# Suffix sums from two f16 halves of the values, with the attention stage's emission weights redrawn

## The chip, the cores and the metric

One core of a Trainium2 chip runs the whole kernel in one launch. The metric is the device time of one execution in microseconds (us). The core has five instruction queues, each worked off in its own order: TensorE (PE: matmuls; its weight loads are listed apart as PEld), VectorE (DVE), ScalarE (ACT), GpSimd (POOL) and SyncE (SP, which here only issues DMA transfers).

## What is computed

One decoder layer on 4 x 1024 tokens of width 512 (16 heads of 32): gated causal self-attention, a retention block on a second input, and a feed-forward block with simulated int8 quantisation, each followed by a residual sum and a layernorm. The change lies in the self-attention:

```python
scores = jnp.einsum('bhqd,bhkd->bhqk', Q, K) / scale
scores = jnp.where(causal[None, None], jnp.asarray(-1000000000.0, x.dtype), scores)
...                                        # head_gates: two small softmaxes of the mean of x
scores = scores * head_gates[:, :, None, None]
attn = jax.nn.softmax(scores, axis=-1)
out = jnp.einsum('bhqk,bhkd->bhqd', attn, V)
```

A masked score is -1e9 times a gate, not minus infinity. When a gate is tiny, the masked (future) keys keep a weight that is the same for all of them, so the kernel needs, beside the ordinary attention, the sum of V over all future keys of each query: the suffix sum of the values.

## The kernel before, in words

The kernel has three stages. In the trace, attention runs to about 1035 us, the retention block follows, and the feed-forward block closes. Only attention is edited.

Attention works in 16 units: 4 batches x 4 groups of 128 channels (4 heads). For each unit:

- **Projection** (`proj_qk` and `proj_v`, from line 554): K, Q and V as three f16 matmuls each (high x high, high x low, low x high; the helper `mm3g`, lines 193 to 199). V is kept in f32, in eight tiles of 128 tokens x 128 channels (line 602). High and low f16 halves of Q and K go to DRAM and come back stacked for the score matmuls (`kst`, `qst`, lines 583 and 591, by SP).
- **Coarse sweep** (`coarse`, lines 620 to 648): scores with f16 halves (`pco`), their maxima by DVE (line 637); one small matmul (`pnm`, line 643) turns the maxima round, and a DMA puts them into `qst` as an extra row, so that the main sweep subtracts them.
- **Suffix sums** (`suffix`, lines 604 to 618): for each pair of token tiles, one f32 matmul per tile with the V tile as weights against `tri_f`, a 128 x 129 triangle of ones with a column of ones at its end (line 611). ACT then adds the running total of the later tiles, tile by tile (line 616), so that each tile waits for the one behind it.
- **Main sweep** (`main`, from line 658), in two halves of 512 queries (g = 0, 1): scores (`pst`, line 703), exponentials on ACT (line 707), product with V (`av`, line 688), and a running sum of the exponentials, mostly on POOL and in some key tiles on DVE (line 693). `corr` (lines 675 to 683) weighs the suffix sums with E, the weight of a masked key; POOL does the product at line 683. The epilogue `ep1` (from line 726) turns the running sum into denominators (`pd`, line 730).

The stage's PSUM tiles take eight banks: three double-bank tiles `st`, shared by `pco`, `pnm`, `pst` and the `pe` of `corr`; one bank `av`; and one bank `mm`, shared by the projections (`pqk`, `pv`), the suffix sums (`psuf`), the output projection (`po`) and the denominators (`pd`).

The order of the work is set in two steps. The Python code runs five generators side by side (`merge`, line 934): `mains`, `coarses` (coarse sweep, then suffix, one unit ahead of `mains`), `all_oprojs`, `others` (sums of x, weights, gates) and `projs`. A generator yields a cost after each piece; the merge always advances the one with the least cost so far divided by its weight (`W_MAIN`, `W_CO`, `W_OP`, `W_X`, `W_PR`). Some yields are only delays (`D_C0` before the first coarse sweep, `D_CO` before each later one, `D_NM` before `pnm`), `C0F` speeds up the first sweep, and `EP1` is how many empty turns stand ahead of an epilogue (line 748). The framework then lays out each engine's queue from that emission order, by its own estimate of when an instruction is ready (`schedule_with_timeline_sim=True`). Engines meet only through semaphores.

The start (`first`, line 774) projects units 0 and 1 and ends with the suffix sums of unit 0.

Of the kernel before, what the change touches and what calls it, by code (L numbers as in the profile page):

```python
# [8 lines left out]
F32 = mybir.dt.float32  # L9
F16 = mybir.dt.float16  # L10
# [3 lines left out]
ALU = mybir.AluOpType  # L14
# [4 lines left out]
P = 128  # L19
B, L, D, H, HD = 4, 1024, 512, 16, 32  # L20
KC = D // P
NT = L // P
# [25 lines left out]
HB = 1  # L48
LOP = "kq"
XLP = 0  # L50
EP1 = 2
D0 = (2,3)
DS = ((), ())
DD = (3,)
# [9 lines left out]
W_OP = 13360.0  # L64
W_OPL = 7700.0
W_CO = 10400.0
D_CO = 1377.0
MTQ = 0
X1Q = 0
ATLP = 0  # L70
NRB = 4
X_S = 215.2
OT = 1
D_C0 = 3876.0
C0F = 4.309
WBY = 250
X_P = 151.7
D_NM = 163.1
W_PR = 20760.0
W_G = 8800.0  # L80
W_X = 10160.0
W_S = 10250.0
W_BE = 11480.0
W_F = 2293.0
W_S1 = 33600.0
# [24 lines left out]
def scaled(gen, f):  # L110
    for cost in gen:
        yield cost / f
# [25 lines left out]
def decoder_kernel(ctx: ExitStack, tc: tile.TileContext, a, c, out):  # L138
    nc = tc.nc
# [95 lines left out]
    xp = ab.enter_context(tc.tile_pool(name="a_x", bufs=1))  # L235
# [113 lines left out]
    with ExitStack() as es:  # L349
        cp = es.enter_context(tc.tile_pool(name="a_c", bufs=1))  # L350
        wk_ = es.enter_context(tc.tile_pool(name="a_w", bufs=2))
        ps = es.enter_context(tc.tile_pool(name="a_ps", bufs=2, space=PSUM))
        st = {}

        def prep(b):
# [3 lines left out]
            for j in range(2):  # L359
                for k in range(KC):  # L360
# [4 lines left out]
                    (nc.gpsimd if XLP else nc.vector).tensor_tensor(out=s["xl"][:, k, tk], in0=xf, in1=s["xh"][:, k, tk], op=ALU.subtract)  # L365
                    yield X_P

# [40 lines left out]
        bo = cp.tile([P, D], F32, name="bo")  # L408
        cnt = cp.tile([P, 2, 16], F32, name="cnt")
        hsel = cp.tile([P, KC, H], F32, name="hsel")  # L410
        tri_f = cp.tile([P, P + 1], F32, name="tri_f")
        future = cp.tile([P, P], BF16, name="future")
        ident_m = cp.tile([P, P], F32, name="ident_m")
        nc.vector.tensor_scalar_mul(ident_m, ident, -1.0 / MS)
# [12 lines left out]

        def consts():
            trib = xp.tile([P, P], F32, tag="xf", name="trib", bufs=2)
            for t, src in (  # L430
                (bsel, c["bsel"]),
                (hsel, c["hsel"]),
                (bq, a["bq"].rearrange("(o p) -> p o", p=P)),
                (tri_f, c["tri"]),
                (trib, c["trib"]),
                (cnt, c["cnt"]),
                (bv, a["bv"].rearrange("(o p) -> p o", p=P)),
                (bo, a["bo"].rearrange("(o n) -> o n", o=1).to_broadcast([P, D])),
            ):
                nc.sync.dma_start(out=t, in_=src)  # L440
            nc.vector.tensor_scalar_mul(future, trib, -1e30)

        g_qs, g_qb, g_gc = (cp.tile([P, B, KC], F32, name=f"g_q{i}") for i in range(3))
        g_gn = cp.tile([P, B, H], F32, name="g_gn")
# [9 lines left out]
        def xsums(b):  # L454
            xs = xp.tile([P, KC, 2], F32, tag="xs2", name="xs2", bufs=2)
            for k in range(KC):
                for j in range(2):
                    xf = xp.tile([P, 512], F32, tag="xf", name="xf", bufs=2)
                    nc.sync.dma_start(out=xf, in_=a["xT"][k * P:(k + 1) * P, b * L + j * 512:b * L + (j + 1) * 512])
                    nc.scalar.activation(xf, xf, AF.Copy, accum_out=xs[:, k, j:j + 1])  # L460
                    yield X_S
            nc.vector.tensor_tensor(out=xsum[:, :, b], in0=xs[:, :, 0], in1=xs[:, :, 1], op=ALU.add)
# [122 lines left out]
        def stack_q(n, g):  # L585
            if len(qst_) < min(n + 1, 2):
                qst_.append(xp.tile([97, 2, 4, 512], F16, tag=f"qst{n}", name=f"qst{n}"))
            b, ot = divmod(n, KC)
            qst = st[b]["qst", ot] = qst_[n % 2]
            for j, w in enumerate((0, 1, 0)):  # L590
                nc.sync.dma_start(out=qst[32 * j:32 * j + 32, g], in_=split_rows("q", n)[w, :, :, g * 512:(g + 1) * 512])

        def proj_v(b, ot):
# [3 lines left out]
            for g in range(2):  # L597
# [3 lines left out]
                    yield from mm3g(p[:, t, :], [lambda k, x_=x_: x_[:, k, tk] for x_ in (s["xh"], s["xl"])], [lambda k, w_=w_: w_[:, k, cs] for w_ in wv], KC, 56)  # L601
                nc.scalar.activation(v[:, 4 * g:4 * g + 4, :], p, AF.Copy, scale=1.0 / WS)

        def suffix(b, ot):
            s = st[b]
            v = s["v", ot]
            suf = s["suf", ot] = xp.tile([P, NT, P + 1], F32, tag="suf", name="suf", bufs=2)
            for t0 in range(NT - 2, -1, -2):
                p = ps.tile([P, 2, P + 1], F32, tag=SUF, name="psuf", bufs=BANKS[SUF])
                for t in range(2):  # L610
                    nc.tensor.matmul(p[:, t, :], lhsT=v[:, t0 + t, :], rhs=tri_f, start=True, stop=True)
                for t in (1, 0):
                    if t0 + t == NT - 1:
                        nc.scalar.copy(suf[:, t0 + t, :], p[:, t, :])
                    else:
                        nc.scalar.activation(suf[:, t0 + t, :], p[:, t, :], AF.Identity, bias=suf[:, t0 + t + 1, P:])
                yield 220
            ready.add((b, ot))

        def coarse(b, ot):  # L620
            s = st[b]
            qst, ks = s["qst", ot], s["kst", ot]
            for half in range(2):
                m = wk_.tile([P, 4, 4, 3], F32, tag="m", name="m", bufs=2)
                nc.scalar.copy(m[:, :, :, 2], gt[b]["gn"][:, 4 * ot:4 * ot + 4].unsqueeze(2).to_broadcast([P, 4, 4]))
                for i in range(4):
                    qt = 4 * half + i
                    for h in range(0, 4, 2):
                        for part in range(1 + half):
                            n = min(512, P * (qt + 1) - 512 * part)  # L630
                            p = ps.tile([P, 2, 512], F32, tag="st", name="pco", bufs=NST)
                            for j in range(2):
                                nc.tensor.matmul(p[:, j, :n], lhsT=qst[0:96, half, h + j, i * P:(i + 1) * P], rhs=ks[0:96, h + j, 512 * part:512 * part + n], start=True, stop=part < half)  # L633
                            if part == half:
                                for j in range(2):
                                    nc.tensor.matmul(p[:, j, n - P:n], lhsT=ident_b, rhs=future, start=False, stop=True)  # L636
                            nc.vector.tensor_reduce(out=m[:, h:h + 2, i, 1 - half + part], in_=p[:, :, :n], axis=AX.X, op=ALU.max)  # L637
                            yield 2 * n * 0.42
                m16 = wk_.tile([P, 4, 4], F32, tag="nm", name="m16", bufs=2)
                nc.vector.tensor_reduce(out=m16, in_=m[:, :, :, 1 - half:], axis=AX.X, op=ALU.max)  # L640
                yield D_NM
                pt = ps.tile([16, P], F32, tag="st", name="pnm", bufs=NST)
                nc.tensor.matmul(pt, lhsT=m16.rearrange("p h t -> p (h t)"), rhs=ident_m, start=True, stop=True)
                mt = wk_.tile([16, P], F16, tag="mt", name="mt", bufs=2)
                nc.scalar.copy(mt, pt)
                (nc.scalar if MTQ else nc.sync).dma_start(out=qst[96:97, half].rearrange("o h (t n) -> o (h t) n", n=P), in_=mt)
                yield 60
                ready.add((b, ot, half))
# [9 lines left out]
        def main(b, ot):  # L658
# [4 lines left out]
            for g in range(2):  # L663
# [83 lines left out]

                pend.extend([lambda: 0] * EP1 + [ep1])
                need[ep1] = (b - 1, 4 * g + 4) if ot == 0 and b else None
# [15 lines left out]
        def unit(n):  # L765
            return divmod(n, KC)
# [7 lines left out]
        def first():  # L774
            yield from proj_qk(0, 0, "k")
            stack_k(0)
            g = hidden0()
            next(g)
            yield from proj_qk(0, 1, "k")
            stack_k(1)  # L780
            for k in range(KC):
                split(wv[0][:, k], wv[1][:, k], wvst[:, k], WS)
            next(g)
            wqst = stage("acc", 2, "wqst")
            nc.sync.dma_start(out=wqst, in_=a["wqT"].rearrange("(k p) n -> p k n", p=P))
            consts()
            yield from proj_v(0, 0)
            for _ in g:
                pass
            split(wq[0], wq[1], wqst, WS)  # L790
            yield from proj_v(0, 1)
            yield from proj_qk(0, 0, "q")
            stack_q(0, 0)
            stack_q(0, 1)
            yield from proj_qk(0, 1, "q")
            stack_q(1, 0)
            stack_q(1, 1)
            yield from suffix(0, 0)

        def second():  # L800
# [5 lines left out]
        def weights_o():  # L806
            for k in range(KC):
                wst = xp.tile([P, 512], F32, tag="xf", name="wst_o", bufs=2)
                nc.sync.dma_start(out=wst, in_=a["woT"][k * P:(k + 1) * P])
                split(wo[0][:, k], wo[1][:, k], wst, WS)  # L810
                yield X_S
            clips()
# [74 lines left out]
        def coarses():  # L887
            yield D_C0
            yield from scaled(coarse(0, 0), C0F)
            for n in range(1, NA):  # L890
                yield from until("main", n - 1)
                yield from until("proj", n + 1)
                if n > 1:
                    stack_k(n)
                    if n == 2:
                        stack_q(n, 0)
                    stack_q(n, 1)
                yield D_CO
                yield from coarse(*unit(n))
                yield from suffix(*unit(n))  # L900

# [50 lines left out]
    with ExitStack() as es:  # L952
        pool = lambda nm: es.enter_context(tc.tile_pool(name=nm, reuse_waits="tile", bufs=2))
        wk_, hp, cp = pool("b_w"), pool("b_h"), pool("b_c")
# [232 lines left out]
    with ExitStack() as es:  # L1187
        cp = es.enter_context(tc.tile_pool(name="c_c", reuse_waits="tile", bufs=1))
        wk_ = es.enter_context(tc.tile_pool(name="c_w", reuse_waits="tile", bufs=2))
# [239 lines left out]
```

## Time and profile before

| what | value |
|---|---|
| time before, median of 3 runs | 1973.27 us (1962.6 to 1976.05) |
| profiled execution, its own time | 1978.85 us |
| its span in the trace | 1977.1 us (1.75 us lie around it) |
| mean granted TensorE clock | 0.979 |
| PE busy | 1832.6 us, 93% of the span, 13456 matmul records |
| DVE / ACT / POOL busy | 1455.4 / 918.2 / 1015.4 us (74 / 46 / 51%) |
| suffix matmuls | 128 instructions, 256 records (f32 leaves two records each) |

PE's records overlap: a `pv` matmul is listed with 0.22 us, and the next one starts 0.06 us after it. So the cost of a matmul on PE is read from the start of one record to the start of the next, not from its duration.

### The profile page before, as it was taken

The page shows a single profiled execution, that of the slowest core. Times are in us where ns is not written, and L with a number is a line of the kernel's source. Part 1 is how long each engine was busy: PE and PEld are TensorE (multiplying, and loading weights), DVE is VectorE, ACT ScalarE, POOL GpSimd, SP SyncE. Part 2 cuts the span into 40 slices and gives each one's busy share as a digit, 9 for nine tenths or more (in the row PEclk, how much of TensorE's full clock was granted, in tenths as well). Part 3 has the DMA queues.
Part 4 walks back from the last instruction along what each step waited for, and adds up shares of the span by engine and source line. Part 5 has one row for each costly group of instructions (what it writes and reads, how often), then busy time and mean ns, then how long its engine had stood idle before and what let it go on. Part 6 is the DMA issues. An engine that isn't in the chain of part 4 may idle for free. (4 is left out here: it accounts for less than half of the span.)

```text
span 1977.1 us, 34827 instructions
## 1 busy us (share of the span) xinstructions
PE 1832.6 (93%) x13456; PEld 968.2 (49%) x13456; DVE 1455.4 (74%) x2455; ACT 918.2 (46%) x1496; POOL 1015.4 (51%) x962
## 2 busy tenths in 40 slices
PE   7689899999999999998889999999999999799996
PEld 4444445444445444554434555555555555344432
DVE  4567766677766777678886777787777767798888
ACT  5655555555555555555553323333223322454375
POOL 1075566756667656766553455445554545200066
PEclk9899999999999999999999999999999999899999
DMA  9612222212123112223137454454545444561076
GB/s 272 192 45 67 82 73 68 84 60 81 54 68 97 62 55 65 73 81 129 44 95 223 136 149 139 147 158 134 153 143 150 120 120 144 176 231 34 0 240 229
DMA packets 149720, 231.00 MB, mean 117 GB/s; under 512 B 34479, under 2 KB 58674, under 8 KB 148914
## 3 DMA queue, kind: packets, MB, share of 16 engines
q1 hardware_dynamic: 148978, 227.72, 38.0%
q8 instruction: 106, 1.74, 0.4%
q10 hardware_dynamic: 576, 1.05, 0.1%
q14 instruction: 60, 0.49, 0.1%
HBM read 156.89 MB, written 71.70 MB: 116 GB/s over the span
## 5 line engine op out<-in xcount | busy, mean ns | idle before, releaser
L693 POOL TENSOR_TENSOR acc<-acc,pt 128x384 f32<-128x384 f32 (+3 forms) x436 | 441.0, 1042 | 244.5 <-ACT pt L707 146.2
L637 DVE TENSOR_REDUCE m<-pco 128x2 f32<-128x1024 f32 (+3 forms) x384 | 356.9, 950 | 128.5 <-PE pco L636 71.3
L707 ACT ACTIVATE pt<-pst 128x1024 f32<-128x1024 f32 (+3 forms) x320 | 240.6, 766 | 179.5 <-PE pst L706 102.4
L633 PE MATMUL pco<-kst,qst 96*128 96x512 f16 (+3 forms) x768 | 186.0, 332 | 28.6 <-DMA qst<-qhl_d 15.7
L703 PE MATMUL pst<-qst,kst 97*128 97x512 f16 (+3 forms) x768 | 187.6, 331 | 9.1 <-DVE m L637 4.9
L1324 POOL TENSOR_TENSOR r<-r,xt 128x512 f32<-128x512 f32 x28 | 38.4, 1383 | 196.2 <-DVE r L1321 186.6
L688 PE MATMUL av<-pt,v 128*32 128x512 f32 (+3 forms) x1280 | 131.0, 482 | 8.7 <-ACT pt L707 7.9
L633 PEld LDWEIGHTS <-qst 96*128 96x128 f16 x768 | 63.7, 99 | 120.2 <-issue 83.7
L1059 POOL TENSOR_TENSOR rs<-var,neghalf 128x16 f32<-128x16 f32 x32 | 93.6, 2925 | 46.9 <-DVE var L1057 26.4
L703 PEld LDWEIGHTS <-kst 97*128 97x128 f16 x768 | 59.4, 98 | 104.0 <-issue 83.2
L1253 PEld LDWEIGHTS <-slab_c 128*128 128x128 bf16 x704 | 68.3, 98 | 78.4 <-issue 1.4
L196 PE MATMUL pqk<-xh,slab_a 128*128 128x512 f16 x256 | 97.1, 384 | 8.7 <-ACT xh L399 5.9
L693 DVE TENSOR_TENSOR acc<-acc,pt 128x512 f32<-128x512 f32 (+3 forms) x102 | 96.5, 963 | 8.7 <-POOL acc L693 4.7
L197 PE MATMUL pqk<-xl,slab_a 128*128 128x512 f16 x256 | 98.0, 383 | 0.0
L198 PE MATMUL pqk<-xh,slab_a 128*128 128x512 f16 x256 | 97.8, 382 | 0.0
L196 PE MATMUL pkv<-slab_b,ch 128*128 128x512 f16 x256 | 97.0, 379 | 0.4 <-DVE dn L732 0.4
L197 PE MATMUL pkv<-slab_b,ch 128*128 128x512 f16 x256 | 97.0, 379 | 0.0
L198 PE MATMUL pkv<-slab_b,cl 128*128 128x512 f16 x256 | 97.0, 379 | 0.0
L1256 ACT ACTIVATE sl<-pw_gate,sgx 128x512 f32<-128x512 f32 x88 | 60.1, 684 | 76.3 <-PE pw_gate L1253 74.7
L196 PE MATMUL pv<-slab_a,xh 128*128 128x128 f16 x512 | 92.0, 221 | 3.4 <-ACT slab_a L170 2.4
L197 PE MATMUL pv<-slab_a,xh 128*128 128x128 f16 x512 | 92.0, 221 | 1.2 <-DVE slab_a L171 1.2
L1020 DVE TENSOR_TENSOR sm<-pst,cmask 128x512 f32<-128x512 f32 x128 | 85.3, 679 | 10.5 <-PE pst L1018 9.2
(299 smaller groups left out, 4595.7 us busy)
## 6 DMA issues: line engine op xcount, KB each, us to landing
xt<-x_d SPq DMA_DIRECT2D x63, 256.0 KB, 3.1
xf<-in_xT_dram SPq DMA_DIRECT2D x48, 256.0 KB, 2.8
kst<-khl_d SPq DMA_DIRECT2D x48, 256.0 KB, 4.0
qst<-qhl_d SPq DMA_DIRECT2D x96, 128.0 KB, 3.8
sk<-qhl_d SPq DMA_DIRECT2D x48, 256.0 KB, 3.8
sk<-khl_d SPq DMA_DIRECT2D x48, 256.0 KB, 4.0
khl_d<-khl SPq DMA_DIRECT2D x16, 512.0 KB, 2.8
xr<-in_x_dram SPq DMA_DIRECT2D x32, 256.0 KB, 2.7
```

Of the source, the lines that this page charges most:

```text
L196: nc.tensor.matmul(ps, lhsT=lh(k), rhs=rh(k), start=k == 0, stop=False)
L197: nc.tensor.matmul(ps, lhsT=lh(k), rhs=rl(k), start=False, stop=False)
L198: nc.tensor.matmul(ps, lhsT=ll(k), rhs=rh(k), start=False, stop=k == n - 1)
L633: nc.tensor.matmul(p[:, j, :n], lhsT=qst[0:96, half, h + j, i * P:(i + 1) * P], rhs=ks[0:96, h + j, 512 * part:512 * part + n], start=True ...
L637: nc.vector.tensor_reduce(out=m[:, h:h + 2, i, 1 - half + part], in_=p[:, :, :n], axis=AX.X, op=ALU.max)
L688: together(nc.tensor.matmul(av[32 * h:32 * h + 32, lo:], lhsT=v[:, kt, 32 * h:32 * h + 32], rhs=pt[:, h, lo:], start=kt == 0, stop=kt == n ...
L693: last["acc"] = eng.tensor_tensor(out=acc[:, h:h + hb, lo:], in0=acc[:, h:h + hb, lo:], in1=pt[:, h:h + hb, lo:], op=ALU.add)
L703: nc.tensor.matmul(p[:, j, lo:], lhsT=ks[:, h + j, kt * P:(kt + 1) * P], rhs=qst[:, g, h + j, lo:], start=True, stop=kt < 4 * g)
L707: last[kt] = nc.scalar.activation(pt[:, h:h + 2, lo:], p[:, :, lo:], AF.Exp)
L1020: nc.vector.tensor_tensor(out=sm, in0=pst, in1=cmask[:, None, :].to_broadcast([P, 4, P]), op=ALU.mult)
L1059: nc.gpsimd.tensor_tensor(out=rs, in0=var, in1=neghalf, op=ALU.pow)
L1253: nc.tensor.matmul(p, lhsT=wT[nm][:, k, i * P:(i + 1) * P], rhs=xqT[g][:, k, :], start=k == 0, stop=k == KC - 1)
```

## The change

The values are split once per unit into a high f16 half (ACT copy) and the remainder in f16 (POOL subtraction), and the suffix matmuls run twice in f16, accumulating in the same bank, against an f16 triangle. `halves` is emitted ahead of the coarse sweep of its unit, and in the start just ahead of the suffix sums of unit 0. The triangle is loaded in f32 into the two-buffer ring `xf`, which the sums of x use too, and copied to f16 by DVE. `vs` has one buffer. Beside it, the merge's costs, delays and weights are redrawn, and one empty turn ahead of each epilogue goes. Nothing uses `W_S`; the other constants are used in the attention stage alone.

```diff
-EP1 = 2
+EP1 = 1
...
-D_CO = 1377.0
+D_VS = 41.83
+D_CO = 1322.0
...
-X_S = 215.2
+X_S = 245.7
...
-D_C0 = 3876.0
-C0F = 4.309
+D_C0 = 6395.0
+C0F = 6.75
...
-X_P = 151.7
-D_NM = 163.1
-W_PR = 20760.0
+X_P = 120.4
+D_NM = 147.5
+W_PR = 19130.0
...
-W_X = 10160.0
-W_S = 10250.0
+W_X = 16350.0
+W_S = 1801.0
...
-        tri_f = cp.tile([P, P + 1], F32, name="tri_f")
+        tri_h = cp.tile([P, P + 1], F16, name="tri_h")
...
             trib = xp.tile([P, P], F32, tag="xf", name="trib", bufs=2)
+            tri = xp.tile([P, P + 1], F32, tag="xf", name="tri", bufs=2)
...
-                (tri_f, c["tri"]),
+                (tri, c["tri"]),
...
+            nc.vector.tensor_copy(tri_h, tri)
...
+        def halves(b, ot):
+            s = st[b]
+            v = s["v", ot]
+            vs = s["vs", ot] = wk_.tile([P, 2, NT, P], F16, tag="vs", name="vs", bufs=1)
+            for g in range(2):
+                tg = slice(4 * g, 4 * g + 4)
+                nc.scalar.copy(vs[:, 0, tg], v[:, tg])
+                nc.gpsimd.tensor_tensor(out=vs[:, 1, tg], in0=v[:, tg], in1=vs[:, 0, tg], op=ALU.subtract)
+                yield D_VS
+
         def suffix(b, ot):
...
-                    nc.tensor.matmul(p[:, t, :], lhsT=v[:, t0 + t, :], rhs=tri_f, start=True, stop=True)
+                    for i in range(2):
+                        nc.tensor.matmul(p[:, t, :], lhsT=vs[:, i, t0 + t, :], rhs=tri_h, start=i == 0, stop=i == 1)
...
             stack_q(1, 1)
+            yield from halves(0, 0)
             yield from suffix(0, 0)
...
                 yield D_CO
+                yield from halves(*unit(n))
                 yield from coarse(*unit(n))
                 yield from suffix(*unit(n))
```

More of the change, by code (lines that the diff above doesn't have):

```diff
@@ L602, in proj_v @@
                 nc.scalar.activation(v[:, 4 * g:4 * g + 4, :], p, AF.Copy, scale=1.0 / WS)
+        def halves(b, ot):
[7 more added lines that the diff above has]
+                yield D_VS
         def suffix(b, ot):
             s = st[b]
-            v = s["v", ot]
+            vs = s["vs", ot]
             suf = s["suf", ot] = xp.tile([P, NT, P + 1], F32, tag="suf", name="suf", bufs=2)
```

## The prediction

> **What bounds the kernel now.** I read the busy times by stage first, to see which engine fills the attention stage (the only one edited); then PE's own waits in it; then the order of time around suffix matmuls, for their price; and last the rows that price the new work on ACT and POOL. The busy times by stage, cut at the start of the first coarse sweep and at the end of attention (columns: stretch, length, PE, PEld, DVE, ACT, POOL busy, granted clock, DMA share, GB/s):
>
> ```profile
> 48.00:61.00 13.00, 1.03 (x11) 0.87 (x10) 2.39 (x5) 7.58 (x17) 0.00 (x0) 0.68 0.89 229
> 61.00:75.00 14.00, 13.62 (x70) 7.84 (x68) 10.68 (x15) 6.64 (x18) 0.00 (x0) 0.81 0.61 197
> 75.00:1035.00 960.00, 898.34 (x7246) 453.57 (x7245) 691.18 (x998) 526.67 (x878) 610.42 (x615) 0.99 0.25 75
> ```
>
> From 75 to 1035 us PE is busy 94% of the time, DVE 72%, POOL 64%, ACT 55%. PE's waits in that stretch are short (who waited for whom: total, times, longest), and all 28 rows together make 58.6 us:
>
> ```profile
> PE pnm L643 <- DVE m L640: 10.3, 8, 3.6
> PE av L688 <- ACT pt L707: 7.9, 18, 1.5
> ...
> PE pco L633 <- DMA kst<-khl_d: 5.3, 6, 1.4
> ...
> PE pco L633 <- DMA qst<-qhl_d: 3.7, 2, 2.0
> ...
> PE pd L730 <- DVE acc L693: 2.4, 3, 1.1
> ...
> PE psuf L611 <- ACT suf L616: 2.3, 3, 1.8
> ...
> PE pd L730 <- POOL acc L693: 0.8, 1, 0.8
> ```
>
> So attention is a queue of matmuls with few holes: a microsecond taken out of PE's queue comes off the end, unless it turns into a new hole. The price of a suffix pair (two tiles, four records) and of a small f16 matmul, from PE's order of time (start, us, group):
>
> ```profile
> 440.35 0.66 PE L611 MATMUL psuf<-tri_f,v 128*128 128x129 f32 x4
> 440.84 0.60 PE L633 MATMUL pco<-kst,qst 96*128 96x512 f16 x2
> ...
> 541.23 0.22 PE L196 MATMUL pv<-slab_a,xh 128*128 128x128 f16 x1
> 541.29 0.22 PE L197 MATMUL pv<-slab_a,xh 128*128 128x128 f16 x1
> 541.34 0.22 PE L198 MATMUL pv<-slab_a,xl 128*128 128x128 f16 x1
> 541.40 0.22 PE L196 MATMUL pv<-slab_a,xh 128*128 128x128 f16 x1
> ```
>
> From start to start the f32 pair takes 440.84 - 440.35 = 0.49 us; one f16 matmul of 128 columns with weights of its own takes (541.40 - 541.23)/3 = 0.056 us. The start-up (same columns):
>
> ```profile
> 47.65 0.61 PE L611 MATMUL psuf<-tri_f,v 128*128 128x129 f32 x4
> 60.23 0.37 PE L633 MATMUL pco<-kst,qst 96*128 96x128 f16 x2 [11.97 <-DMA qst<-qhl_d]
> ```
>
> Here one pair of unit 0 lies in front of a wait of 11.97 us for a transfer, and costs nothing.
>
> **The suffix matmuls, units 1 to 15.** 15 units x 4 pairs = 60 pairs. Each goes from 0.49 us to four f16 matmuls, 4 x 0.056 = 0.22 (129 columns as against 128 adds nothing I can read). 60 x 0.27 = 16.2 us off PE's queue. Lower bound: the start-to-start of a record inside the group, (440.84 - 440.35)/4 = 0.12 us, may hold some 0.01 us of switching to the next group; with 0.45 per pair the gain is 13.8. Upper: 0.50 per pair (a second pair stands from 564.56 to 565.06) gives 16.8.
>
> The Trainium skill speaks against this price: "TensorE: Matmul & The Clock Gate", section "Back-to-back issue gap", gives about 81 ns per matmul as the sustained spacing at 128 columns once each has its weight load, and 56 ns only for the isolated gap. By 81 ns the pair would cost 0.32 and the gain would be 60 x 0.17 = 10 us. The row of this trace has weights of its own for each `pv` matmul and still shows 0.056, so the row stands.
>
> **Unit 0.** Pairs 2 and 3 run at the low clock of the second row above (0.81), 0.96 us each (61.68 to 62.64 and 64.14 to 65.10 in the same order of time), pair 4 takes 0.50: 2.4 us outside the wait. In the built queue of the changed kernel two pairs stand ahead of the first coarse matmul, not one; the other two cost 2 x 0.22 to 2 x 0.45. Gain 1.7 us (0 if the wait shrinks with it).
>
> **ACT.** 32 copies of 128x512 from f32 to f16. The row of the same shape is 0.61 us:
>
> ```profile
> L567 ACT CAST khl<-qk 128x512 f16<-128x512 f32 x27 | 16.5, 612 | 0.2
> L568 POOL TENSOR_TENSOR khl<-qk,khl 128x512 f16<-128x512 f32 x26 | 32.1, 1233 | 38.5 <-ACT khl L567 38.5
> ```
>
> 32 x 0.61 = 19.5 us on an engine that is 55% busy. But place matters. `vs` has one buffer, so the copies of unit n+1 need the last suffix matmul of unit n, and in the built ACT queue both copies stand as a pair just before the last additions of unit n's totals, with exponentials next behind. The single `mm` bank comes free, and the exponentials run, up to 1.22 us later. Behind the suffix pair, PE has score or value matmuls that do not need that bank. Bounds: 0 (all hidden) to 19.5 us (each copy in full). I take 5, nearer to 0, because PE waited for the suffix additions 3 times in 60 (2.3 us) and for exponentials 7.9 us in all.
>
> **POOL.** 32 subtractions x 1.23 us = 39 us on an engine 64% busy. In the built queue the two of a unit stand together, 24 or more coarse tiles ahead of the first suffix matmul that reads them, so PE does not wait for them. Who stands behind them: the weighting of the previous unit's suffix sums (line 683), Q and K remainders and the running sums. Exponentials of 1024 wait for PE (lines 703 and 706), and in this stretch for POOL only once, 1.4 us, so the pool of `pt` buffers has slack. I take 0; if that cover went, each pair would hold `pt` or a denominator back by up to 2.5 us. As a bound I add 3 us (the 3.2 us that PE waits for the running sum at `pd`, once more).
>
> **Triangle.** The load has the same 128x129 f32; DVE gets one copy of it, less than the 0.69 us of its 128x512 f16 rows, once, beside PE. The transfer now goes through the `xf` ring, and in the built SP queue the first load of x for the sums stands behind both triangles and two weight loads, the next ones behind more stack loads. ACT takes these sums in turn with Q's halves, whose store and load end the 11.97 us wait. A load of x lands 3.0 us after its issue: the wait can end 3 us earlier or later. I take 0.
>
> **The redrawn weights.** All units are emitted in another order; no row prices that directly. From the built PE queues I counted matmuls (without suffix) between two events, which needs no time. From the last value product of a half to its denominators: more in 18 of 32 cases, fewer in 10; places with under 10 in between go from 9 to 5 of the 32, and the least from 2 to 4, although the empty turn is gone (`EP1`). From the last coarse tile to `pnm`: two places with 0 become 4; longer in three more units (up to 60). From the last score matmul of unit n-2 to the coarse sweep that needs its buffers: 24 to 39 before, 24 to 79 after. On the other side the suffix ends later against the next coarse sweep (some of its tiles stand ahead of the last pair in 10 units, 7 before), so `corr` gets its totals later. `D_CO` plus two `D_VS` is 1405.7 against 1377: nothing. Bounds: all waits for `pnm`, `pd` and the stack loads gone, 10.3 + 3.2 + 5.3 + 3.7 = 22.5 us off, or as much again on. I take 4 off: the 3.2 at `pd` and some of `pnm`.
>
> **The sum.** -16.2 - 1.7 + 5 + 0 + 0 - 4 = -16.9, say -17. The profiled execution took 1978.85 us, so 1962 there; it lies 5.6 above the median of 1973.27, and against the median the forecast is 1956.3 us. The retention and feed-forward stages are not edited; only their queues shift by readiness.
>
> **The rivals.**
> A, the forecast: PE's saving arrives, the rest nearly cancels. Own range 1948 to 1966 (ACT 0 to 10, redraw -8 to 0).
> B, the redraw also closes holes: three quarters of the 22.5 us go. -17.9 - 16.9 + 5 = -30: 1943.5. For it: the counts above. Against: half of the holes come from DVE and DMA, which lose no work.
> C, the saving is given back on ACT: every copy delays the exponentials in full. -17.9 - 4 + 19.5 = -2.4: 1971. For it: the place of the pair in the queue. Against: ACT is idle 45% of the stage, mostly waiting for PE.
> D, slower: the same pair of copies holds the only `mm` bank and one exponential behind it, and PE's next matmul on that bank stands at the head of its queue. Price per unit 1.22 + 1.02 (an exponential of 1024) = 2.24 us, x 15 = 33.6; -17.9 - 4 + 33.6 = +11.7: 1985. It decides from (17.9 + 4)/15 = 1.5 us per unit on. Against: PE has other matmuls to run between.
>
> **How the numbers follow.** A 0.50, B 0.22, C 0.19, D 0.09. A measurement of this kernel tells about 1% (19.7 us) from no change: under 1953.5 is faster, above 1993 slower. Faster: nearly all of B (0.20) and the lower part of A (0.16), 0.36. Slower: the part of D whose price passes 2.8 us per unit, and a start-up or redraw at its upper bound, 0.06. Within: 0.58. The range 1938 to 1980 holds A, most of B and C, and leaves out D above 1980 and the redraw at its full lower bound with the copies hidden (-17.9 - 22.5 = 1933).
>
> **What would show it.** Right: suffix records start 0.056 us apart and their PE busy time shrinks; attention ends about 17 us earlier; PE's waits stay near 59 us; the subtractions are never what `psuf` waits for. Wrong: `psuf` 0.08 us or more apart; new waits of PE for `suf` or `pt` near the copies, of 1 us per unit (C) or over 1.5 (D); a wait before the first `pco` that is 3 us longer or shorter; or retention and feed-forward differing by more than 3 us.

## The result, and the profile after

The changed kernel takes **1987.52 us** (median of 5 runs, 1984.42 to 1992.52). Against runs of before on the same chip the ratio is 1.0087 (95% interval 1.0066 to 1.0107): 0.9% slower, some 17 us (the two medians, 1973.27 and 1987.52, lie 14 us apart). The forecast was 1956.3 us, and the range ended at 1980. The profiled execution of after took 1984.42 us; that of before, 1978.85, lies 8 us above the medians of before beside the experiments (1969.3 to 1971.5 us), so two single traces are compared with care below.

The busy line of the page of after:

```profile
PE 1822.1 (92%) x13432; PEld 950.2 (48%) x13456; DVE 1472.6 (74%) x2456; ACT 931.6 (47%) x1528; POOL 1048.5 (53%) x994
```

PE lost 10.5 us of busy time; some of it is not saved but missing, since 24 matmul records fewer are listed, and the last stage, where nothing was edited, lacks about as many. ACT and POOL, which got the copies and the subtractions, gained 13.4 and 33.1 us. The line to notice is DVE: 17.2 us more (1455.4 before), with one instruction more. Something made DVE's old instructions last longer.

Busy times by stage, after (same columns as before, attention now ends at 1047):

```profile
48.00:61.00 13.00, 0.69 (x6) 0.32 (x3) 2.85 (x5) 7.95 (x20) 0.00 (x0) 0.62 0.70 207
61.00:75.00 14.00, 10.89 (x65) 6.33 (x66) 11.02 (x14) 6.34 (x15) 3.24 (x2) 0.86 0.64 206
75.00:1047.00 972.00, 893.42 (x7256) 438.53 (x7254) 707.13 (x1001) 539.29 (x907) 638.45 (x644) 0.98 0.24 74
```

In attention PE is busy 5 us less than before and the stretch is 12 us longer. PE's waits in it, over all rows, are some 77 us, where they were 58.6. Summed by the engine that ended them, those for DVE grew most, from 25.9 to 39.0 us; those for ACT went from 22.4 to 29.1. The largest:

```profile
PE pnm L657 <- DVE m L654: 11.7, 9, 2.3
PE av L702 <- ACT pt L721: 11.4, 19, 2.8
PE pst L717 <- DVE m L651: 7.3, 15, 1.1
PE pco L647 <- DVE m L651: 5.7, 16, 1.0
```

No row stands out as a new wait: matmuls of the main and coarse sweeps wait a little more often for exponentials and for DVE's maxima. The suffix matmuls cost what was forecast, 65.45 - 65.23 = 0.22 us per pair (order of time on PE):

```profile
65.23 0.39 PE L625 MATMUL psuf<-tri_h,vs 128*128 128x129 f16 x4
65.45 0.38 PE L647 MATMUL pco<-kst,qst 96*128 96x512 f16 x1
```

Behind attention, where nothing was edited, this trace of after is 6.5 us shorter than that of before (935.6 against 942.1 us). The prediction had named a difference of more than 3 us there as a sign of being wrong. Two traces can differ by that without a cause in the change: with the same queues, the stretch of 475 us behind attention took 472.1 us in e14 below and 480.6 in e15.

### The profile page after: what moved, and what is told of

Its sections match the earlier page's. It is cut to its first block, busy times and chain, and to the rows that moved or that the text cites. A ratio compares the mean times of both kernels' runs of the same rounds, so it can differ in the third digit from the quotient of the medians.

```text
span 1982.6 us, 34876 instructions
## 1 busy us (share of the span) xinstructions
PE 1822.1 (92%) x13432; PEld 950.2 (48%) x13456; DVE 1472.6 (74%) x2456; ACT 931.6 (47%) x1528; POOL 1048.5 (53%) x994
## 3 DMA queue, kind: packets, MB, share of 16 engines
q10 hardware_dynamic: 576, 1.05, 0.1%
## 5 line engine op out<-in xcount | busy, mean ns | idle before, releaser
L707 POOL TENSOR_TENSOR acc<-acc,pt 128x384 f32<-128x384 f32 (+3 forms) x436 | 433.5, 1024 | 186.9 <-ACT pt L721 172.6
L707 DVE TENSOR_TENSOR acc<-acc,pt 128x1024 f32<-128x1024 f32 (+3 forms) x102 | 105.2, 1044 | 10.2 <-POOL acc L707 7.0
L1036 DVE TENSOR_TENSOR sm<-pst,cmask 128x512 f32<-128x512 f32 x128 | 85.2, 681 | 10.5 <-PE pst L1034 10.2
```

Source lines behind the costliest of these rows:

```text
L707: last["acc"] = eng.tensor_tensor(out=acc[:, h:h + hb, lo:], in0=acc[:, h:h + hb, lo:], in1=pt[:, h:h + hb, lo:], op=ALU.add)
L1036: nc.vector.tensor_tensor(out=sm, in0=pst, in1=cmask[:, None, :].to_broadcast([P, 4, P]), op=ALU.mult)
```

## The experiments

First came the parts of the change and prices of single operations, each with the queues that the framework lays out for it. They contradicted each other, and the layout itself turned out to move the time (e11 and e15); the last six therefore hold before's queues. In the cuts from the code, the bookkeeping around a call is left out. Ratios are to before on the same chip.

### Which part costs: halves or weights

```diff
 # e1: the halves, and all old constants
-D_CO = 1322.0
+D_CO = 1377.0 - 2 * D_VS
 # e2: f32 suffix sums as before, and all new constants
-D_CO = 1377.0
+D_CO = 1322.0 + 2 * 41.83
 # e3: the changed kernel with two empty turns
-EP1 = 1
+EP1 = 2
 # e4: the changed kernel with the old D_C0, C0F, W_X and X_S
```

> The f16 halves and the f16 suffix matmuls with every emission constant of the kernel before (the delay ahead of a coarse sweep is 1377 less the two costs that the halves yield, so the merge places the same pieces as before). Theory R (the redrawn order is what cost time): the suffix saving of 14 to 16 us arrives here, 1955 to 1962 us against 1973. Theory H (the halves' work on ACT and POOL is what cost time, the order is neutral): about as slow as the changed kernel, 1983 to 1990 us.

> The f32 suffix matmuls of the kernel before with every emission constant of the changed kernel (the delay is 1322 plus the two costs that the halves yield). Theory R: the order alone costs 25 to 30 us, so 1998 to 2003 us. Theory H: near the kernel before, 1968 to 1978 us.

> The changed kernel with two empty turns ahead of an epilogue again, all else as changed. Theory R with the denominators at fault: most of the loss comes back, 1965 to 1975 us. Theory R with another constant at fault, or theory H: within 4 us of the changed kernel, 1983 to 1991 us.

> The changed kernel with the four constants of the start and of the sums of x as before (first delay, speed of the first coarse sweep, weight of the other work, cost of a sum of x). Theory R with the start at fault: the 10 us by which the first masked-key weights came later go away, 1975 to 1979 us. Otherwise within 4 us of the changed kernel.

| run | median us | ratio (95%) |
|---|---|---|
| e1: halves, old constants | 1984.95 | 1.0072 (1.0056 to 1.0087) |
| e2: f32, new constants | 1970.38 | 1.0001 (0.9989 to 1.0013) |
| e3: changed kernel, two turns | 1979.53 | 1.0046 (1.0032 to 1.0061) |
| e4: changed kernel, old start | 1991.72 | 1.0103 (1.0086 to 1.0119) |

The redrawn weights alone change nothing that can be measured. The halves are slower in all four orders of emission (e1, the change itself, e3, e4), by 9 to 20 us.

### What in the halves costs

```diff
 # e5: old constants; halves made once, all units read unit 0's
-            vs = s["vs", ot]
+            vs = st[0]["vs", 0]
 # e6: old constants; halves made and not read
-                    for i in range(2):
-                        nc.tensor.matmul(p[:, t, :], lhsT=vs[:, i, t0 + t, :], rhs=tri_h, start=i == 0, stop=i == 1)
+                    nc.tensor.matmul(p[:, t, :], lhsT=s["v", ot][:, t0 + t, :], rhs=tri_f, start=True, stop=True)
 # e7: e1 without the subtraction, one f16 matmul per tile
 # e8: e1 with the subtraction on DVE
-                nc.gpsimd.tensor_tensor(out=vs[:, 1, tg], in0=v[:, tg], in1=vs[:, 0, tg], op=ALU.subtract)
+                nc.vector.tensor_tensor(out=vs[:, 1, tg], in0=v[:, tg], in1=vs[:, 0, tg], op=ALU.subtract)
 # e9: e1 with the copies on POOL
-                nc.scalar.copy(vs[:, 0, tg], v[:, tg])
+                nc.gpsimd.tensor_copy(vs[:, 0, tg], v[:, tg])
```

> Old emission constants, f16 suffix matmuls, but the halves are made once, for unit 0, and all 16 units multiply unit 0's halves (their suffix sums are those of unit 0; the rest is computed in full). So PE has the f16 price and ACT and POOL have 30 copies and 30 subtractions less. Theory P (PE bounds attention, the work on ACT and POOL is what cost time): the saving of 14 to 16 us arrives, 1955 to 1958 us against 1971. Theory F (the shorter suffix is worth nothing or less, since PE's queue only gets more holes or a lower clock): 1969 to 1985 us.

> Old emission constants, the f32 suffix matmuls of the kernel before, and the 32 copies and 32 subtractions as work whose output nobody reads. Theory P: PE does all it did, and the copies and subtractions cost their full 28 to 30 us, 1998 to 2002 us. Theory F: the same work costs little, 1971 to 1978 us. In between, both have a part.

> Old emission constants, f16 suffix from the high half alone: 32 copies on ACT, no subtraction, one f16 matmul per tile (the remainder of the values is left out of the suffix sums). Theory POOL (the subtractions are what cost time): 1948 to 1958 us. Theory ACT (the copies are): within 8 us of the f16 halves at old constants, 1976 to 1985 us.

> Old emission constants, f16 halves, the subtraction on DVE (0.69 us a piece by its rows) in place of POOL (1.16 us). Theory POOL: most of the loss goes, 1958 to 1972 us. Theory ACT: 1980 to 1990 us, since the copies stay and DVE, at 72% of the stage, gets 22 us more.

> Old emission constants, f16 halves, both the copies and the subtractions on POOL, none on ACT. Theory A (the 19.5 us of copies on ACT are what cost time, and PE's saving is worth nothing): 1970 to 1976 us against 1971. Theory W (any new link between V and the suffix costs it, on whatever engine): 1980 to 1986 us.

| run | median us | ratio (95%) |
|---|---|---|
| e5: halves once | 1973.92 | 1.0009 (0.9988 to 1.0029) |
| e6: halves unread | 1981.22 | 1.0065 (1.0041 to 1.0089) |
| e7: high half only | 1983.81 | 1.0082 (1.0054 to 1.0110) |
| e8: subtraction on DVE | 1978.90 | 1.0058 (1.0035 to 1.0080) |
| e9: copies on POOL too | 2000.97 | 1.0161 (1.0140 to 1.0183) |

e5 is the first surprise: the saving on PE, taken nearly alone, is worth nothing. e9 suggests that work is dearest on POOL: in its trace the stack loads of K came late, and PE's largest wait is

```profile
PE pco L647 <- DMA kst<-khl_d: 21.4, 10, 2.7
```

But e7 adds no work to POOL at all and is as slow as e1, which speaks for ACT's copies.

### Is PE, or ACT, the bound

```diff
 # e10: before, each f32 suffix matmul twice
-                    nc.tensor.matmul(p[:, t, :], lhsT=v[:, t0 + t, :], rhs=tri_f, start=True, stop=True)
+                    for i in range(2):
+                        nc.tensor.matmul(p[:, t, :], lhsT=v[:, t0 + t, :], rhs=tri_f, start=i == 0, stop=i == 1)
 # e11: before, one ACT copy per pair in place of the two chained additions
+                nc.scalar.copy(suf[:, t0:t0 + 2, :], p)
 # e12: e2 with EP1 = 2
```

> The kernel before with every f32 suffix matmul run twice into the same bank (the suffix sums come out doubled): 128 more f32 matmuls, 29 to 31 us of PE time, nothing else. If attention were bound by PE's queue: 1996 to 2002 us. If PE has room at these places, as the halves made once suggest: 1971 to 1980 us. In between, PE binds in one direction: added time counts, time taken away doesn't.

> The kernel before with one ACT copy per suffix pair in place of two chained additions (the running totals over token tiles are left out): 64 instructions in place of 128, some 18 to 22 us less on ACT, PE as before. Theory A in its strong form (ACT binds attention both ways): 1956 to 1962 us. If ACT's additions were covered and only the place of the copies costs: 1967 to 1972 us.

> The f32 suffix with the redrawn constants, but two empty turns ahead of an epilogue. The return of the second turn was worth 8 us to the changed kernel. If that gain belongs to the order alone: 1962 to 1966 us, faster than both kernels. If it belongs to the halves (their pair on ACT near the denominators): 1968 to 1973 us.

| run | median us | ratio (95%) |
|---|---|---|
| e10: suffix twice | 2006.74 | 1.0180 (1.0163 to 1.0197) |
| e11: one copy per pair | 1988.38 | 1.0084 (1.0060 to 1.0108) |
| e12: f32, new constants, two turns | 1968.53 | 0.9985 (0.9972 to 0.9998) |

Time added on PE arrived (some 30 us of matmuls, 36 us of end); time taken off it did not (e5). And e11, which takes work off ACT and adds none anywhere, costs 17 us. No theory of a busy engine explains that. What e11 shares with e1 and e7 is that the framework laid out its queues anew. So up to here each run had two causes in it, its work and its layout; that goes for e10's 36 us too.

### The same queues

For these six, every instruction that before also has keeps before's place on each of the five queues. An edge that orders two instructions of one engine, without a wait, ties each to its predecessor in before's queue:

```diff
+    for e, steps in order.items():          # before's queue of engine e
...
+            tc.add_manual_dep(k, before.name, mybir.DependencyInfo(mybir.DependencyClass.NoSync, mybir.DependencyReason.DATA), reason="the same queues")
+            before = k
```

Only added instructions stand between them: the second f16 matmul behind the first, the copies and the subtractions, in e13's places (e16 has its own). The f32 triangle keeps a tile of its own beside the f16 one.

> The halves of the change with all old constants, as in the first experiment, but with every instruction that before also has held in before's order on each of the five queues; only the added copies, subtractions and second matmuls stand between them (the f32 triangle keeps a tile of its own). Against 1971 us of before. Theory L (the loss comes from the queues being laid out anew, not from the work): the saving on PE arrives less the small delays of ACT, 1956 to 1966 us. Theory W (the halves' own work costs it, whatever the order): 1982 to 1988 us, as in the first experiment.

> As in the experiment with the halves made once (only unit 0's halves are made, and all units use them, so the suffix sums of the other units are wrong), but with before's order held on each queue. This is the saving on PE alone. Theory L: 13 us less than before, 1955 to 1961 us, since nothing but the suffix matmuls changes. Theory W': PE's time at the suffix matmuls is not what sets the end, so 1970 to 1974 us again.

> As in the experiment with one ACT copy per suffix pair (the running totals are left out), but with before's order held on each queue. It takes about 20 us of ACT work away and a chain of waits. Theory L: 1966 to 1972 us, no slower than before. Theory W'': the timing of ACT alone throws the engines against each other, and it stays at 1985 us or more.

> Before's f32 suffix sums, and the halves made but read by nothing, with before's order held on each queue: the price of the added work of ACT and POOL alone. Theory L: 1971 to 1976 us (the 5 us that the prediction gave ACT, or less). Theory W: 1980 to 1984 us, as without held queues.

Two further runs split e13, in its places:

```diff
 # e17: copies for all units, subtractions for unit 0 alone
+                if (b, ot) == (0, 0):
+                    nc.gpsimd.tensor_tensor(out=once[:, tg], in0=v[:, tg], in1=vs[:, tg], op=ALU.subtract)
 # e18: subtractions for all units, copies for unit 0 alone
+                if (b, ot) == (0, 0):
+                    nc.scalar.copy(once[:, tg], v[:, tg])
+                nc.gpsimd.tensor_tensor(out=vs[:, tg], in0=v[:, tg], in1=once[:, tg], op=ALU.subtract)
```

> The halves with before's order held on each queue, and with ACT's copies in the same places as there, but POOL's subtractions made for unit 0 alone: the other units read unit 0's low half, so their suffix sums are wrong. Beside the run with halves made once (1969.6 us, no copies and no subtractions) and the one with all halves (1987.7 us, both) this is the corner with copies alone. Theory S (a copy pair delays PE by about 0.6 us at its place, and POOL's subtractions make DVE's small addition to the denominators last up to 4 us in three places): 15 x 0.6 = 9 us over the corner without either, 1976 to 1981 us, and no such addition over 1.5 us. Theory C (the copies are all of it): 1985 us or more. Theory N (neither alone): 1970.

> The other corner: POOL's subtractions for every unit in the same places, ACT's copies for unit 0 alone, whose high half the other units read and subtract (their suffix sums are wrong). Theory S: the three long additions of DVE stay (3.7 to 4.0 us where they last 0.2 to 0.7 without the subtractions), each with the wait of PE behind it, 3 x 3 = 9 us and what half clock adds: 1978 to 1983 us. Theory C: 1970 to 1972 us, subtractions hidden.

| run, before's queues | ACT copies | POOL subtractions | suffix | median us | ratio (95%) |
|---|---|---|---|---|---|
| e14: halves once | unit 0 | unit 0 | f16 | 1969.63 | 1.0004 (0.9987 to 1.0021) |
| e17: copies only | all | unit 0 | f16 | 1972.97 | 1.0018 (1.0003 to 1.0033) |
| e18: subtractions only | unit 0 | all | f16 | 1984.29 | 1.0087 (1.0064 to 1.0111) |
| e13: halves | all | all | f16 | 1987.66 | 1.0093 (1.0069 to 1.0117) |
| e16: halves unread | all | all | f32 | 1977.39 | 1.0037 (1.0020 to 1.0055) |
| e15: one copy per pair | none | none | f32 | 1970.03 | 0.9999 (0.9982 to 1.0016) |

Three things are settled by this table.

**The layout alone moves the time by as much as the change.** e15 issues the same instructions as e11 and takes 17 to 18 us less. So e7, and every comparison of two layouts, can't be read as a price.

**POOL's subtractions are most of the loss.** They cost 14.7 us without the copies (1984.29 - 1969.63) and 14.7 us with them (1987.66 - 1972.97). These pairs of runs stand on different chips (e13, e14 and e17, e18); by the ratios to before on each chip it is 16 and 15 us, with some 6 us of uncertainty. The copies cost 3.3 us by the medians and 1 to 3 by the ratios, which is not clear of the noise. Theory S named the right part: e18 came out 1.3 us above its range, and e17 3 us below, since it put the copies too high (9 us).

**The saving on PE is worth nothing even when nothing else changes** (e14). For Theory L this was the miss: it had 1955 to 1961.

How a subtraction on POOL reaches the end, in the traces. DVE's small addition that completes the denominators (a tile's row: count, then least, median and longest duration in ns), in before, e14, e18 and the changed kernel:

```profile
L733 DVE TENSOR_TENSOR dn<-dn,ec x32: 150/176/1036, 112.5 to 1036.4; 128x16 f32<-128x16 f32 x32
```

```profile
L748 DVE TENSOR_TENSOR dn<-dn,ec x32: 150/176/886, 110.7 to 1032.2; 128x16 f32<-128x16 f32 x32
```

```profile
L751 DVE TENSOR_TENSOR dn<-dn,ec x31: 151/176/3968, 111.6 to 1010.7; 128x16 f32<-128x16 f32 x31
```

```profile
L747 DVE TENSOR_TENSOR dn<-dn,ec x31: 147/175/2392, 116.8 to 1015.9; 128x16 f32<-128x16 f32 x31
```

The same 128x16 instruction lasts 0.18 us or 3.97 us. One of the long ones in e18, in DVE's order of time and, below it, POOL's:

```profile
511.94 3.97 DVE L751 TENSOR_TENSOR dn<-dn,ec 128x16 f32<-128x16 f32 x1
515.84 0.70 DVE L699 TRANSPOSE_TENSOR_REDUCE ec<-E 128x16 f32<-128x512 f32 x1
516.46 0.20 DVE L752 RECIPROCAL dn<-dn 128x16 f32<-128x16 f32 x1
516.60 0.62 DVE L655 TENSOR_REDUCE m<-pco 128x2 f32<-128x512 f32 x1
```

```profile
505.20 2.27 POOL L617 TENSOR_TENSOR vs<-v,once 128x512 f16<-128x512 f32 x2
507.43 2.38 POOL L711 TENSOR_TENSOR acc<-acc,pt 128x256 f32<-128x256 f32 x5
509.76 1.17 POOL L571 TENSOR_TENSOR khl<-qk,khl 128x512 f16<-128x512 f32 x1
510.88 3.87 POOL L711 TENSOR_TENSOR acc<-acc,pt 128x384 f32<-128x384 f32 x4
514.70 1.18 POOL L701 TENSOR_TENSOR suf<-suf,E 128x512 f32<-128x512 f32 x1
516.61 0.22 POOL L700 TENSOR_TENSOR ec<-ec,cnt 128x16 f32<-128x16 f32 x1 [0.73 <-DVE ec L699]
```

From 505.20 to 515.88 POOL's queue has no gap. The addition, which reads two operands from SBUF as POOL's do, starts at 511.94 and ends at 515.91, the moment that POOL runs dry. Behind it on DVE's queue stands a maximum of the coarse sweep (516.60) that frees a score bank, and PE waits for that:

```profile
515.79 0.28 PE L654 MATMUL pco<-future,ident_b 128*128 128x128 bf16 x2
517.27 0.38 PE L721 MATMUL pst<-qst,kst 97*128 97x256 f16 x2 [1.21 <-DVE m L655]
517.49 0.28 PE L724 MATMUL pst<-ident_b,future 128*128 128x128 bf16 x2
519.21 0.38 PE L721 MATMUL pst<-qst,kst 97*128 97x256 f16 x2 [1.45 <-DVE m L655]
```

In e14, with the same queues and no subtraction there, the same addition lasts 0.37 us (DVE, then POOL):

```profile
507.78 0.37 DVE L748 TENSOR_TENSOR dn<-dn,ec 128x16 f32<-128x16 f32 x1
508.07 0.70 DVE L696 TRANSPOSE_TENSOR_REDUCE ec<-E 128x16 f32<-128x512 f32 x1
```

```profile
505.03 1.16 POOL L571 TENSOR_TENSOR khl<-qk,khl 128x512 f16<-128x512 f32 x1 [1.05 <-ACT khl L570]
506.15 3.87 POOL L708 TENSOR_TENSOR acc<-acc,pt 128x384 f32<-128x384 f32 x4
```

It ends at 508.15, about where POOL's second addition gives way to the third (506.15 + 2 x 0.97 = 508.09). In e18 two such places inside the four additions and one behind them went by unused. POOL's rows ahead of this show a difference. In e14 its queue has a gap of 1.05 us ahead of 505.03, 2.75 us before the addition. In e18 the two subtractions (2.27 us) stand there, the gap is gone, and POOL's run without a gap had begun 17.5 us before the addition:

```profile
494.42 10.83 POOL L711 TENSOR_TENSOR acc<-acc,pt 128x512 f32<-128x512 f32 x11 [5.02 <-ACT pt L725]
```

Over the traces of all twenty kernels here, twelve additions of this row lasted longer than 1.4 us, and each came after a POOL run of 17.5 us or more without a gap. They are in e1, e3, e4, e13, e18 and the changed kernel, all with subtractions on POOL. Beside a younger run the addition lasted 1.32 us at most. A long run is not enough: in e13, after 20.5 us of one, the addition at 462.8 took 0.70 us. Why is not shown.

PE's two score matmuls come in e14 with no wait listed:

```profile
511.73 0.38 PE L718 MATMUL pst<-qst,kst 97*128 97x256 f16 x2
511.95 0.28 PE L721 MATMUL pst<-ident_b,future 128*128 128x128 bf16 x2
512.37 0.38 PE L718 MATMUL pst<-qst,kst 97*128 97x256 f16 x2
```

Since e14 and e18 issue the same matmuls in the same order, PE's start times can be set side by side: e18 falls behind by 2.9 us between 260 and 280 us, by 4.8 between 500 and 540 and by 4.5 between 740 and 780, the three places with a long addition (3.96, 3.97 and 3.84 us). That is 12.2 us of the 13.5 us by which the two spans differ; the other steps, of up to 3 us, go both ways. Between e17 and e13, again with the same order, the same three places give 5.6, 4.6 and 4.2 us of 17.1. PE's waits for DVE in attention say the same: 26.2 us in e14 and 26.0 in e17, 36.0 in e18 and 35.1 in e13. Part of it follows from the waits: at the second and third place PE's clock is halved for 3.4 us behind them (512-column matmuls 0.38 to 0.42 us apart from 519.94 on, 0.215 before).

"SBUF — State Buffer", section "Who interferes with whom", of the Trainium skill has a mechanism for this: VectorE and GpSimd share a port pair, and an instruction of VectorE with two SBUF inputs can't run beside one of GpSimd that reads SBUF. The trace agrees in kind. It goes further in size: the addition was held through four POOL instructions, not for the rest of one.

e16, with the same POOL work and f32 suffix sums, has no long addition at these places (0.67, 0.71 and 0.22 us) and costs 7.4 us, not 18. Its subtractions stand elsewhere on POOL's queue, and the POOL run that these additions meet is 2.4 to 2.9 us old. So the price of a subtraction is not fixed. Whether its place or the longer suffix matmuls make the difference is not separated here.

Where e14's saving goes can be read pair by pair. Before, then e14, at the same place in the queue:

```profile
445.17 0.66 PE L611 MATMUL psuf<-tri_f,v 128*128 128x129 f32 x4
446.32 0.64 PE L688 MATMUL av<-pt,v 128*32 128x256 f32 x8 [0.49 <-ACT pt L707]
```

```profile
442.62 0.39 PE L624 MATMUL psuf<-tri_h,vs 128*128 128x129 f16 x4
443.71 0.64 PE L703 MATMUL av<-pt,v 128*32 128x256 f32 x8 [0.71 <-ACT pt L722]
```

From the pair to the value product it is 1.15 us before and 1.09 in e14: the exponential sets that start, and 0.22 of the 0.27 us saved turn into a longer wait. A slot is the time from the start of a matmul to the start of the next. Set against e15, whose suffix sums are f32 and whose queues are the same (it has less work on ACT), e14's slots of the suffix matmuls are 12.7 us shorter over attention (from 75 to 1035 us of e15), and those of score, value and coarse products 12.1 us longer. Set against the trace of before, 8 us above its medians, they are 13.2 us shorter and 7.6 longer.

## Why the prediction was wrong, step by step

- **The suffix matmuls, -16.2 and -1.7.** The price was right: 0.22 us per pair and some 13 us less in the slots of the suffix matmuls. (By the 81 ns of "TensorE: Matmul & The Clock Gate" in the Trainium skill, section "Back-to-back issue gap", the pair would have been 0.32, an estimate; 55 ns per matmul is measured.) That it "comes off the end, unless it turns into a new hole" was not: with the order held, none of it arrives (e14, -3 to +4 us by its interval). This was the first failing step. A PE that is busy 94% of a stage isn't yet the bound of it. At the pair shown, the suffix matmuls were work that PE did while it would have waited for an exponential. That the whole stage goes at the pace of the loop through ACT's exponentials and DVE's maxima is an inference; taking 18 us of work off ACT (e15) didn't make it faster either. "PE's waits stay near 59 us" was the test named for this, and they rose to 77.
- **ACT, +5.** Measured 1 to 3 us, not clear of the noise (e17 less e14, e13 less e18): not contradicted. PE's waits for exponentials, from which the 5 was chosen, were 12.2 us over all rows, not 7.9, which is one row. Rival C and rival D, which put the loss on these copies, gave 1971 and 1985; D came within 3 us of the time with the wrong cause.
- **POOL, "I take 0", with a bound of 3.** The second failing step: some 15 us with the queues held. I looked for who waits for the subtractions, and nobody does. What I didn't ask is who shares a resource with POOL: DVE's busy time rises by 17.2 us in the changed kernel, with one instruction more. The row was there in before: the addition `dn<-dn,ec` lasted from 0.15 to 1.04 us with the same shape. The description of the kernel says that engines meet only through semaphores; these rows show one slowed by another where no wait on a semaphore is listed.
- **The redrawn weights, -4.** Measured 0 with f32 suffix sums (e2: -2 to +3 us by its interval). Rival B fell with it.
- **Triangle and start, 0.** The first coarse matmul starts at 61.29 us, 60.23 before: 1 us, within what was left open.

By these measures the sum would have been 0 + 3 + 15 + 0 = +18 us, which is what e13 measured. That the change has +17 with queues of its own may be chance. In e13 the causes are shown. In the changed kernel itself only the total is: its queues differ from before's, its longest additions are 2.39 and 2.15 us, and at the first of them PE had a projection in hand and didn't stop. PE's waits for DVE grew there by 13 us, but in e7, with nothing added on POOL and a layout of its own, they are 33.8 us too, and it is as slow. DVE's busy time doesn't tell the two apart either: it is 1472.6 us in the changed kernel, 1472.7 in e13 and 1475.5 in e18, but also 1464.0 in e14, which lost nothing, and 1462.4 in e1, which lost 14 us. How much of the 17 us is contention and how much is the new layout stays open, and so does what in e11's layout costs 17 us. Of the versions run, e12 is the fastest (ratio 0.9985); its gain of 0.15% is hardly more than its interval.

## What to carry to other kernels

A high busy share doesn't make an engine the bound: ask of the instruction you shorten what ends the next wait behind it, and if that is another engine, the saving can stay in the wait. When you put work on an engine that is half idle, ask not only who waits for the result, but whose instructions slow down while it runs, and whether the work fills the gaps in that engine's queue; rows of one shape with widely spread durations show the first beforehand. Where a framework lays out the queues, hold them when you compare two versions, or you measure the layout too.

## What the runs showed of the hardware

- An addition of 128x16 on DVE took 3.97 us instead of 0.18 while POOL worked off a run of instructions on SBUF tiles that had had no gap for 17.5 us, and ended when that run did (e18 at 511.94; e13 has the same).
- PE's clock fell to half for 3.4 us after two waits of 1.21 and 1.45 us with 0.5 us of matmuls between them (e18, 515.9 to 519.2 us).
- The same instructions in two orders differ by 17 to 18 us, 0.85% (ratios 1.0084 and 0.9999, e11 and e15), although the named waits in attention sum to only some 60 us (62.8 and 55.7).
